# Another order for one attention kernel's engine queues, with PSUM banks named one by one

## The chip, the cores and the metric

The kernel runs on one core of a Trainium2 chip. The metric is device time in microseconds of the whole program. The kernel before takes 495.95 us (median of 3 runs, 495.19 to 496.17).

A core has five engines, each with its own instruction queue that it works off in order. TensorE (PE in the profile) multiplies matrices, and its weight loads are listed as PEld. VectorE (DVE), ScalarE (ACT) and GpSimd (POOL) do the elementwise work. SyncE (SP) only starts DMA transfers here. An engine waits for another by a semaphore. Matrix products land in PSUM, which this kernel holds as eight banks of 128 x 512 float32; everything else lies in SBUF.

## The reference

All data is float32. `x` is 2 x 2048 x 640, the context 2 x 154 x 1024: 77 text rows and 77 image rows per batch. 20 heads of width 32.

```
q    = heads(x @ Wq.T)
k, v       = heads(text @ Wk.T),    heads(text @ Wv.T)
k_ip, v_ip = heads(ip @ Wk_ip.T),   heads(ip @ Wv_ip.T)
out  = softmax(q k.T / sqrt(32)) v  +  softmax(q k_ip.T / sqrt(32)) v_ip
y    = merge(out) @ Wo.T + bo + x
```

The two softmaxes are separate: each row of 154 scores is two rows of 77, each with its own maximum and sum.

## The kernel before

Everything is held transposed, channels on the partitions. The 640 channels are five chunks of 128, and a chunk holds four heads of 32. A chunk of one batch is one `q` number from 0 to 9, and it is cut in two halves of 1024 tokens, so there are 20 units `u`. The 1024 tokens of a unit are eight tiles of 128 tokens, and these are taken in three groups `s` of 3, 3 and 2 tiles (`GROUPS`).

The order of all work is one list, `SCHEDULE`. Each word emits a few instructions, and each engine gets its own in the order of the list. A word is a kind, its numbers and, behind `@`, a place. The kinds that matter here:

- `q.u.h@bank`: the query product of a unit's half block, ten matmul records on line 206; `cq.u.h`: ScalarE copies it out of the bank, scaled (line 220).
- `k.c.t@bank`, `v.c.t@bank`: keys and values of a chunk (line 144); `ck`, `cv` copy them out. `LK.n` loads one block of 512 KB of their weights into slot n modulo 4; weight block n is read by product n, which is 4c + t for k and 4c + 2 + t for v.
- `Rs.u@place`: the scores of group s of unit u (line 242). Four heads run beside each other on 32 rows of the array each, and head g writes bank g of the four that the place names. A three-tile group is 24 matmul records, a two-tile group 16.
- `Ks.u`: ScalarE copies the four banks to SBUF (line 254), head by head. `M`: VectorE's row maxima (line 290, or 293 out of PSUM). `S`: GpSimd subtracts them (line 304). `E`: ScalarE's exponential (line 310). `D`: VectorE's row sums (line 315). `I`: their reciprocals (line 320). `N`: GpSimd multiplies by them (line 325). `T`: VectorE transposes (line 332).
- `A.q@place`: attention times values for a chunk, 160 records on line 341, four banks; `CA.q` copies it out.
- `m`, `o`, `p`, `z`, `F`: products of the output projection (lines 499, 509, 480, 887); `cm`, `co`, `Y`, `yz` add them to sums on VectorE; `G`, `W`, `V`, `X` are sums of operands on GpSimd or VectorE; `SF`, `SS`, `LX`, `LQ`, `LO`, `VS`, `LA`, `LW` are transfers on the sync queue. The projection of the second batch stands at the end of the list, behind A.9.

Three sets say which groups take another way. A group in `BIASED` or `DIRECT` has no subtraction: its exponential is computed row by row on ScalarE, with the negated maximum as a bias (line 278), 24 instructions for a three-tile group and 16 for a two-tile one. A `DIRECT` group is not copied either: its maxima and exponentials read the banks. In `SUMMED` groups the exponentials add up the row sums themselves, and there is no `D`.

Before, the eight banks were two halves of four, and R and A named a half:

```
halves = banks[:G], banks[G:]
...
if k[0] == "R":
    at[name] = halves[int(where)]
    scores(x, i, at[name])
```

In front of the list stand the first loads, five warming matmuls, the query products of units 0 and 2 and the keys of chunk 0, in banks 4, 5, 2 and 7. They are the same in both kernels.

Of the kernel before, what the change touches and what calls it, by code (L numbers as in the profile page):

```python
# [9 lines left out]
F32 = mybir.dt.float32  # L10
# [10 lines left out]
def kernel(  # L21
# [43 lines left out]
        (11, 0), (12, 0), (13, 0), (13, 2), (14, 0), (14, 2), (15, 1), (15, 2), (18, 1), (19, 2),  # L65
    }
    BIASED = {
        (2, 2), (3, 2), (4, 2), (6, 2), (8, 2), (9, 2), (11, 2), (12, 1), (16, 2), (17, 2), (18, 2),
    }
    SUMMED = {  # L70
        (4, 2), (11, 2), (12, 0), (13, 0), (13, 2), (14, 0), (15, 1), (15, 2), (16, 2), (17, 2), (18, 1),
        (18, 2), (19, 2),
# [13 lines left out]
    halves = banks[:G], banks[G:]  # L86
# [183 lines left out]
    def exponential_of(u, s, ps=None, den=None):  # L270

        n = GROUPS[s][1]
        for g in range(G):
            for t in range(n):
                for x in range(2):
                    row = rows_of(u, s)[:, t * G + g, x]
                    one = t * G + g, slice(x, x + 1)
                    nc.scalar.activation(  # L278
                        row,
                        row if ps is None else rows_in(ps[g], n)[:, t, x],  # L280
                        AF.Exp,
                        bias=maxs[(u, s)][:, *one],
                        accum_out=None if den is None else den[:, *one],
                    )
# [300 lines left out]
    for t in range(2):  # L585

        ps = halves[t][G - 2 + t]
        project_kv(t, ps)
        for b in range(B):
            nc.scalar.copy(kT[:, 0, b, t, :], keys_in(ps)[:, b])  # L590
# [73 lines left out]
    def emit(word):  # L664
        name, _, where = word.partition("@")
        k, *args = name.split(".")
        x, y = (*(int(a) for a in args if a.isdigit()), None, None)[:2]
        i = int(k[1:]) if k[1:].isdigit() else None
        if k[0] == "R":
            at[name] = halves[int(where)]  # L670
            scores(x, i, at[name])
        elif k == "A":
            at[name] = halves[int(where)]
# [262 lines left out]
```

## Time and profile before

| | |
|---|---|
| median of 3 runs | 495.95 us (495.19 to 496.17) |
| span of the profiled execution, first to last instruction | 494.6 us (no other time of this execution is given) |
| TensorE busy | 489.1 us, 99% of the span |
| VectorE busy | 413.9 us, 84% |
| GpSimd busy | 370.5 us, 75% |
| ScalarE busy | 309.5 us, 63% |
| DMA | 69.38 MB, mean 140 GB/s |

How to read it: busy times of engines overlap, so only the engine that others wait for sets the time. The chain of waits follows the program back from its last instruction and names at each step what released it. In the rows of that chain a piece is a run of instructions of one line that follow each other without a wait.

### The profile page before, as it was taken

To read this page: it belongs to the slowest core of one execution; us is meant where nothing else is said; L and a number is where in the kernel's file an instruction comes from. 1 tells how busy PE (TensorE), PEld (TensorE's weight loads), DVE (VectorE), ACT (ScalarE), POOL (GpSimd) and SP (SyncE) were. 2 spreads that over 40 slices of the span, in tenths; PEclk is the share of its full clock that TensorE was granted. 3 is DMA by queue.
4 is the path that set the end of the run, shared out by engine and by line. 5 is a ranking of instruction groups with operands and counts; after the bars stand their busy time and mean duration, and the time that the engine had idled before them with its cause. 6 is when DMAs were issued, how large, how long until landed. Compare 5 with 4: busy or idle time off the path is not lost.

```text
span 494.6 us, 10484 instructions
## 1 busy us (share of the span) xinstructions
PE 489.1 (99%) x4116; PEld 287.7 (58%) x4116; DVE 413.9 (84%) x416; ACT 309.5 (63%) x1002; POOL 370.5 (75%) x158
## 2 busy tenths in 40 slices
PE   9999999999999999999999999999999999999997
PEld 5666648558557556456566654754755675444443
DVE  0069989989899989979988896687789898999996
ACT  1275788977687778677899786587889862100000
POOL 0069988988988988879886758475689899798700
PEclk9999999999999999999999999999999999999999
DMA  8992046203241724895540666455550212320125
GB/s 278 350 288 80 17 124 181 67 1 95 62 150 44 247 65 146 270 345 178 161 172 27 215 195 223 134 172 183 184 169 19 90 42 85 129 85 2 42 85 212
DMA packets 67105, 69.38 MB, mean 140 GB/s; under 512 B 5488, under 2 KB 47088, under 8 KB 67056
## 3 DMA queue, kind: packets, MB, share of 16 engines
q1 hardware_dynamic: 66048, 67.54, 43.7%
q10 hardware_dynamic: 1008, 1.18, 0.7%
q8 instruction: 32, 0.52, 0.4%
q14 instruction: 17, 0.14, 0.1%
HBM read 54.94 MB, written 10.49 MB: 132 GB/s over the span
## 4 chain that ended last, share of the span: by engine, by line
PE 96%; DMA 3%; ACTq 0%; ACT 0%; DVE 0%; DVEq 0%; issue 0%
PE bank L206 34%; PE bank L887 12%; PE bank L341 11%; PE bank L242 11%; PE bank L499 10%; PE bank L144 9%; PE bank L480 7%; PE bank L509 3%; DMA aT<-in_L_xattn_Wk_ip_dram 2%; DMA x<-in_x_dram 1%; ACTq L538 0%; ACT pb L254 0%; ACTq L552 0%; DVE acc L830 0%; DVEq L931 0%
## 5 line engine op out<-in xcount | busy, mean ns | idle before, releaser
L325 POOL TENSOR_TENSOR pb<-pb,rden 128x1848 f32<-128x1848 f32 (+1 forms) x60 | 176.0, 2943 | 30.4 <-DVE rden L320 23.6
L304 POOL TENSOR_TENSOR pb<-pb,mx 128x1848 f32<-128x1848 f32 (+1 forms) x39 | 121.6, 3129 | 55.4 <-DVE mx L290 55.3
L206 PE MATMUL bank<-x,wq 128*128 128x512 f32 x280 | 125.4, 598 | 0.1
L332 DVE STREAM_TRANSPOSE pb<-pb 128x1920 f32<-128x1920 f32 (+1 forms) x60 | 115.9, 1938 | 9.1 <-POOL pb L325 8.9
L290 DVE TENSOR_REDUCE mx<-pb 128x24 f32<-128x1848 f32 (+1 forms) x50 | 91.6, 1844 | 32.1 <-ACT pb L254 31.9
L254 ACT COPY pb<-bank 128x462 f32<-128x462 f32 (+1 forms) x200 | 85.3, 542 | 29.3 <-PE bank L242 28.9
L315 DVE TENSOR_REDUCE den<-pb 128x24 f32<-128x1848 f32 (+1 forms) x47 | 88.9, 1895 | 15.6 <-ACT pb L310 12.8
L206 PEld LDWEIGHTS bank<-x,wq 128*128 128x128 f32 x280 | 51.7, 190 | 60.0 <-issue 58.8
L310 ACT ACTIVATE pb<-pb 128x1848 f32<-128x1848 f32 (+1 forms) x39 | 65.6, 1684 | 17.5 <-POOL pb L304 17.4
L278 ACT ACTIVATE pb<-bank,mx 128x77 f32<-128x77 f32 x208 | 60.4, 387 | 6.5 <-DVE mx L293 6.5
L278 ACT ACTIVATE pb<-pb,mx 128x77 f32<-128x77 f32 x184 | 54.1, 356 | 1.9 <-DVE mx L290 1.8
L341 PE MATMUL bank<-pb,v 32*32 32x512 f32 x1600 | 55.2, 597 | 0.0
L206 PE MATMUL bank<-x,aT 128*128 128x512 f32 x116 | 51.8, 596 | 0.0
L242 PEld LDWEIGHTS bank<-kT,qT 32*128 32x128 f32 x1024 | 36.1, 184 | 21.6 <-issue 13.3
L144 PE MATMUL bank<-wo_ct,aT 128*128 128x154 f32 x320 | 46.0, 297 | 0.7 <-DMA aT<-in_L_xattn_Wk_ip_dram 0.4
L144 PEld LDWEIGHTS bank<-wo_ct,aT 128*128 128x128 f32 x320 | 43.0, 188 | 4.7 <-issue 3.0
L242 PE MATMUL bank<-kT,qT 32*128 32x154 f32 x1024 | 45.1, 305 | 0.0
L278 ACT ACTIVATION_READ_ACCUMULATOR pb<-bank,mx 128x1 f32 x168 | 44.0, 266 | 0.0
L341 PEld LDWEIGHTS bank<-pb,v 32*32 32x32 f32 x1600 | 29.0, 103 | 22.7 <-issue 10.1
L480 PE MATMUL bank<-aT,wo_ct 128*128 128x512 f32 x80 | 36.3, 595 | 0.0
L206 PEld LDWEIGHTS bank<-x,aT 128*128 128x128 f32 x116 | 21.4, 190 | 23.7 <-issue 23.5
L220 ACT ACTIVATE qT<-bank 128x512 f32<-128x512 f32 x32 | 19.3, 631 | 23.4 <-PE bank L206 23.4
(83 smaller groups left out, 524.2 us busy)
## 6 DMA issues: line engine op xcount, KB each, us to landing
x<-in_x_dram SPq DMA_DIRECT2D x20, 1280.0 KB, 6.7
out_dram<-acc SPq DMA_DIRECT2D x19, 256.0 KB, 2.9
x<-in_x_dram SPq DMA_DIRECT2D x17, 256.0 KB, 5.9
acc<-in_x_dram SPq DMA_DIRECT2D x16, 256.0 KB, 4.4
out_dram<-x SPq DMA_DIRECT2D x15, 256.0 KB, 2.0
v<-vS SPq DMA_DIRECT2D x160, 20.0 KB, 2.7
aT<-in_L_xattn_Wk_dram SPq DMA_DIRECT2D x5, 512.0 KB, 6.0
aT<-in_L_xattn_Wk_ip_dram SPq DMA_DIRECT2D x5, 512.0 KB, 5.5
```

Source lines behind the costliest of these rows:

```text
L144: nc.tensor.matmul(keys_in(out), loaded[n][:, k, :], cT[:, k, :, t, :], start=(k == 0), stop=(k == NCC - 1))
L206: nc.tensor.matmul(pq, weight_of(q)[:, k, :], xs[place_of(u, h)][:, k, :], start=(k == 0), stop=(k == NC - 1), skip_group_check=loose,)
L242: nc.tensor.matmul(ps[g][:, ts(t, 2 * L)], qTs[(u, h)][g * D : (g + 1) * D, ts(st, P)], kT[g * D : (g + 1) * D, c, b].rearrange("p t l -> ...
L254: nc.scalar.copy(keys_of(u, s)[:, :, g], ps[g][:, : n * 2 * L].rearrange("p (n l) -> p n l", n=n))
L278: nc.scalar.activation(row, row if ps is None else rows_in(ps[g], n)[:, t, x], AF.Exp, bias=maxs[(u, s)][:, *one], accum_out=None if den i ...
L290: nc.vector.tensor_reduce(mx, rows_of(u, s), AX.X, ALU.max, negate=negate)
L304: nc.gpsimd.tensor_tensor(rows_of(u, s), rows_of(u, s), maxs[(u, s)].unsqueeze(3).to_broadcast([P, n, 2, L]), ALU.subtract)
L315: nc.vector.tensor_reduce(den_of(u, s), rows_of(u, s), AX.X, ALU.add)
L325: nc.gpsimd.tensor_tensor(rows_of(u, s), rows_of(u, s), rdens[(u, s)].unsqueeze(3).to_broadcast([P, n, 2, L]), ALU.mult)
L332: nc.vector.transpose(p, p)
L341: nc.tensor.matmul(pa[r][g * D : (g + 1) * D, :], v4s[q % 2][rows, g, k, :], zones[rows, :, g, k, :], start=(k == 0), stop=(k == NK - 1),)
L480: nc.tensor.matmul(ps, wo[:, k, ts(NC - 1, P)], rows_of_attention(b, k)[:, i], start=(k == 0), stop=(k == NC - 1),)
```

## The change

The diff does four things. `SCHEDULE` is another order of the words. R and A name four banks one by one (`R0.0@6452`: head 0 in bank 6, head 1 in 4, head 2 in 5, head 3 in 2) where they named a half. The exponential of a group is four words, one for each head g; for a row-by-row group each emits a quarter of the instructions, for a plain group the first emits the one instruction and the other three emit nothing. And `DIRECT`, `BIASED` and `SUMMED` hold other groups. Pairs of R words next to each other on TensorE go from 14 to 16.

```diff
     DIRECT = {
-        (11, 0), (12, 0), (13, 0), (13, 2), (14, 0), (14, 2), (15, 1), (15, 2), (18, 1), (19, 2),
+        (1, 2), (15, 1), (17, 1), (19, 2),
     }
     BIASED = {
-        (2, 2), (3, 2), (4, 2), (6, 2), (8, 2), (9, 2), (11, 2), (12, 1), (16, 2), (17, 2), (18, 2),
+        (3, 2), (5, 2), (7, 2), (9, 2), (11, 1), (12, 1), (13, 2), (14, 1), (14, 2), (15, 2), (18, 0), (19, 0),
     }
     SUMMED = {
-        (4, 2), (11, 2), (12, 0), (13, 0), (13, 2), (14, 0), (15, 1), (15, 2), (16, 2), (17, 2), (18, 1),
-        (18, 2), (19, 2),
+        (1, 2), (3, 2), (5, 2), (11, 1), (12, 1), (13, 2), (14, 2), (15, 1), (17, 1), (18, 0), (19, 0), (19, 2),
     }
...
-    def exponential_of(u, s, ps=None, den=None):
+    def exponential_of(u, s, g, ps=None, den=None):
...
-        for g in range(G):
-            for t in range(n):
-                for x in range(2):
+        for t in range(n):
+            for x in range(2):
...
-        "q.0.1@5 R0.0@0 cq.0.1 R1.0@1 K0.0 SF.0.0 q.1.0@0 K1.0 M0.0 LK.4 LQ.5 LK.5 M1.0 S0.0 R2.0@1 v.0.0@1 K2.0 "
-        "cq.1.0 S1.0 M2.0 E0.0 v.0.1@5 D0.0 q.1.1@7 LK.7 S2.0 E1.0 LK.6 I0.0 D1.0 N0.0 E2.0 cv.0.0 cv.0.1 R0.1@0 "
-        "I1.0 cq.1.1 D2.0 R1.1@1 K0.1 N1.0 T0.0 k.1.0@0 K1.1 I2.0 M0.1 q.2.1@3 N2.0 T1.0 S0.1 M1.1 R2.1@1 k.1.1@1 "
...
+        "R0.0@6452 q.0.1@7 K0.0 M0.0 cq.0.1 S0.0 q.1.0@2 E0.0.0 E0.0.1 cq.1.0 R1.0@6457 R2.0@0132 K1.0 E0.0.2 "
+        "v.0.1@6 v.0.0@7 K2.0 M1.0 M2.0 S1.0 q.1.1@2 R0.1@5013 E1.0.0 cv.0.0 cv.0.1 cq.1.1 R1.1@4762 K0.1 E0.0.3 "
+        "K1.1 LK.6 SF.0.3 LK.5 k.1.1@5 R2.1@0134 S2.0 D0.0 E2.0.0 E1.0.1 q.3.0@6 E1.0.2 E2.0.1 E1.0.3 I0.0 SQ.0 "
...
+        "LK.12 v.2.0@2 VS.1.0 E0.3.2 cq.5.0 E1.3.1 E0.3.3 K2.4 E1.3.2 E1.3.3 cv.2.0 R1.4@5473 D0.3 R0.4@6012 I2.3 "
...
+        "E0.4.3 E2.4.2 cv.2.1 k.3.1@6 K0.5 D0.4 ck.3.1 E1.4.3 E2.4.3 R2.5@7452 I0.4 D1.4 R1.5@0136 N0.4 SQ.2 I1.4 "
...
         if k[0] == "R":
-            at[name] = halves[int(where)]
+            at[name] = [banks[int(n)] for n in where]
             scores(x, i, at[name])
...
                 elif direct or biased:
-                    exponential_of(
-                        x, i, ps if direct else None, den_of(x, i) if (x, i) in SUMMED else None
-                    )
-                else:
+                    if (x, i) in SUMMED and (x, i) not in dens:
+                        den_of(x, i)
+                    exponential_of(x, i, int(args[1]), ps if direct else None, dens.get((x, i)))
+                elif args[1] == "0":
                     exponential(x, i)
```

More of the change, by code (lines that the diff above doesn't have):

```diff
@@ L85 @@
     banks = [psum.tile([P, TB], F32, name=f"bank_{n}") for n in range(2 * G)]
-    halves = banks[:G], banks[G:]
     wqs = [const.tile([P, NC, P], F32, name=f"wq_{n}") for n in range(3)]
@@ L268, in den_of @@
         return dens[(u, s)]
-    def exponential_of(u, s, ps=None, den=None):
+    def exponential_of(u, s, g, ps=None, den=None):
         n = GROUPS[s][1]
-        for g in range(G):
-            for t in range(n):
-                for x in range(2):
[L276 to L283, printed above, removed]
-                    )
+        for t in range(n):
+            for x in range(2):
+                row = rows_of(u, s)[:, t * G + g, x]
+                one = t * G + g, slice(x, x + 1)
+                nc.scalar.activation(
+                    row,
+                    row if ps is None else rows_in(ps[g], n)[:, t, x],
+                    AF.Exp,
+                    bias=maxs[(u, s)][:, *one],
+                    accum_out=None if den is None else den[:, *one],
+                )
     def maxima(u, s, ps=None, negate=False):
@@ L585 @@
     for t in range(2):
-        ps = halves[t][G - 2 + t]
+        ps = banks[G * t + G - 2 + t]
         project_kv(t, ps)
@@ L669, in emit @@
         if k[0] == "R":
-            at[name] = halves[int(where)]
+            at[name] = [banks[int(n)] for n in where]
             scores(x, i, at[name])
         elif k == "A":
-            at[name] = halves[int(where)]
+            at[name] = [banks[int(n)] for n in where]
             attend(x, at[name])
@@ L701, in emit @@
                 elif direct or biased:
-                    exponential_of(
-                        x, i, ps if direct else None, den_of(x, i) if (x, i) in SUMMED else None
-                    )
-                else:
+                    if (x, i) in SUMMED and (x, i) not in dens:
+                        den_of(x, i)
+                    exponential_of(x, i, int(args[1]), ps if direct else None, dens.get((x, i)))
+                elif args[1] == "0":
                     exponential(x, i)
```

136 rows, old and new, of the table SCHEDULE are left out of this document.

## The prediction, made before the changed kernel was run

> **What bounds the kernel now.** I read the page's busy times first, then the waits of TensorE, then the chain of waits in order of time. The page:
>
> ```profile
> span 494.6 us, 10484 instructions
> PE 489.1 (99%) x4116; PEld 287.7 (58%) x4116; DVE 413.9 (84%) x416; ACT 309.5 (63%) x1002; POOL 370.5 (75%) x158
> ...
> DVE  0069989989899989979988896687789898999996
> ...
> PEclk9999999999999999999999999999999999999999
> ...
> PE 96%; DMA 3%; ACTq 0%; ACT 0%; DVE 0%; DVEq 0%; issue 0%
> ```
>
> The waits of TensorE, all of which lie before the ordered list begins at 19.37 us:
>
> ```profile
> PE bank L573 <- DVE pb L571: 1.1, 1, 1.1
> PE bank L144 <- DMA aT<-in_L_xattn_Wk_ip_dram: 0.4, 1, 0.4
> PE bank L144 <- DMA wo_ct<-in_ctx_dram: 0.3, 1, 0.3
> ```
>
> So the matmul queue sets the end, at full clock, and no other engine matters until TensorE waits for it. What a new order is worth can then come from two things only: how long the same matmuls take in another sequence, and the waits in that sequence. The number of matmuls does not change: both lists hold the same 232 TensorE words (60 R, 10 A, 38 q, 18 k or v, 40 m, o, p and z, 66 F). The chain of waits, by pieces of one line, shows how the sequence matters (start, length, line, records; the record counts are a little short in places):
>
> ```profile
> 19.37 4.29 PE bank L206 x10
> 23.66 1.78 PE bank L242 x48
> 25.45 4.49 PE bank L206 x10
> 29.94 0.74 PE bank L242 x16
> 30.67 4.41 PE bank L144 x32
> 35.09 4.29 PE bank L206 x10
> ...
> 63.21 1.00 PE bank L242 x24
> ...
> 68.69 5.45 PE bank L341 x150
> 74.15 1.00 PE bank L242 x24
> 75.14 4.41 PE bank L144 x32
> 79.56 1.52 PE bank L242 x40
> 81.08 2.31 PE bank L144 x16
> ...
> 210.51 5.45 PE bank L341 x150
> 215.96 4.49 PE bank L206 x10
> ```
>
> L206 is a query word, L242 score words, L144 key and value words, L341 the product with the values. A run of scores costs 0.78 us for each group of three tiles (1.78 − 1.00) and 0.22 us once more for the run (1.00 − 0.78; for two tiles 0.74 is 0.52 + 0.22). A full-width word behind scores costs 0.20 us more than behind another full-width word: 4.49 against 4.29, and 4.41 for two k or v words where the one behind full-width work is 2.10 (4.41 − 2.31). Behind L341 it is the same (215.96 starts where an attention word ends, and takes 4.49). L341 itself is 5.45 us, and scores behind it pay their 0.22 (1.00 at 74.15).
>
> **Part 1, fewer changes between narrow and full-width work: −1.24 us.** I counted neighbours in the two lists. The 60 score words form 46 runs before (14 of them pairs) and 44 after (16 pairs): 2 × 0.22 = 0.44 us. Stretches of full-width words that follow scores or an A word: 50 before (45 behind scores, 5 behind A), 46 after (42 and 4): 4 × 0.20 = 0.80 us. It is more than two pairs alone would give because one more A now stands directly behind scores and one more R directly behind an A. Bounds: −0.84 (only the two pairs count, 0.42 each) to −1.24. I take −1.24, since every row of each kind above has the same price.
>
> **Part 2, waits inside pairs: −0.55 us.** A pair of a two-tile and a three-tile group is 40 records and takes 1.52 us where nothing holds it. Five such pairs take longer:
>
> ```profile
> 91.96 1.74 PE bank L242 x38
> ...
> 129.06 1.74 PE bank L242 x38
> ...
> 166.16 1.75 PE bank L242 x40
> ...
> 228.53 1.67 PE bank L242 x39
> ...
> 273.35 1.76 PE bank L242 x40
> ```
>
> Together that is 0.22 + 0.22 + 0.23 + 0.15 + 0.24 = 1.06 us. In the first three the second group uses the bank of the query word just before the pair (R0.4 after q.5.0@6, R0.6 after q.7.0@6, R0.8 after q.9.0@4), so ScalarE's copy of the queries is not done when the second group comes. The new list names four banks for each word. R2.6@0167 no longer touches the bank of q.7.0@3, but R0.8 still meets that of q.9.0@1, and R2.0 and R1.1 those of q.1.0@2 and q.1.1@2. Nothing in the trace tells how many waits the other banks bring. Bounds: −1.06 (none left) to 0 (as many). I take half.
>
> **Part 3, the beginning: +1.05 us.** Three waits are new, and each is read from the first words of the new list.
>
> First, R0.0 moves ahead of q.0.1. It reads the keys that ScalarE copies from the bank of the last k product:
>
> ```profile
> 19.41 0.35 ACT L590 COPY kT<-bank 128x77 f32<-128x77 f32 x2 [2.47 <-PE bank L144]
> ```
>
> The matmuls are through at 19.37 and the copies at 19.76. Before, q.0.1 covered that (4.29 us); now the whole TensorE queue stands behind R0.0 for 0.4 us (0.3 if the first copy, that of this batch, is enough; 0.5 with a handover).
>
> Second, R1.0 and R2.0 are joined behind q.1.0, and R2.0 needs q.1.0's bank, so cq.1.0 must be done. On ScalarE E0.0 stands ahead of it. R0.0 starting at 19.76 gives K0.0 about 1.9 us of copies (4 × 64.7/136) from 20.85, then the row maximum, the subtraction and the exponential by these rows:
>
> ```profile
> L254 ACT COPY pb<-bank 128x462 f32<-128x462 f32 x136 | 64.7, 590 | 16.6 <-PE bank L242 16.6
> L254 ACT COPY pb<-bank 128x308 f32<-128x308 f32 x64 | 22.1, 440 | 12.7 <-PE bank L242 12.4
> L290 DVE TENSOR_REDUCE mx<-pb 128x24 f32<-128x1848 f32 x34 | 69.5, 2049 | 29.4 <-ACT pb L254 29.3
> L304 POOL TENSOR_TENSOR pb<-pb,mx 128x1848 f32<-128x1848 f32 x33 | 108.3, 3289 | 54.5 <-DVE mx L290 54.5
> L304 POOL TENSOR_TENSOR pb<-pb,mx 128x1232 f32<-128x1232 f32 x6 | 13.5, 2255 | 0.9 <-DVE mx L290 0.8
> L310 ACT ACTIVATE pb<-pb 128x1848 f32<-128x1848 f32 x33 | 58.1, 1765 | 16.7 <-POOL pb L304 16.6
> L220 ACT ACTIVATE qT<-bank 128x512 f32<-128x512 f32 x32 | 19.3, 631 | 23.4 <-PE bank L206 23.4
> ```
>
> 20.85 + 1.9 + 2.05 + 3.29 + 1.77 + 0.63 = 30.49, and 0.1 us of handovers: 30.6. TensorE reaches R2.0 at 19.76 + 1.00 + 4.49 + 4.29 + 0.90 = 30.44. That is 0.15 us of wait (0 to 0.4). The same counting for R1.1 behind cq.1.1 gives 0, with 0.2 as its other end.
>
> Third, the weights of k.1.1. The old list issues LK.4, LQ.5 and LK.5 early; the new one begins its sync queue with LK.6, SF.0.3, LK.5. LK.6 overwrites what v.0.0 reads, so the sync queue, and LK.5 in it, stands until v.0.0 has run. The old list has such loads right behind the v words too (LK.7 and LK.6, issues first, then KB and us to landing):
>
> ```profile
> 35.12 0.37 SPq L134 DMA_DIRECT2D aT<-in_L_xattn_Wv_ip_dram  x1
> 35.54 0.57 SPq L134 DMA_DIRECT2D aT<-in_L_xattn_Wv_dram  x1
> ...
> aT<-in_L_xattn_Wv_ip_dram SPq DMA_DIRECT2D x1, 512.0 KB, 4.2
> ...
> aT<-in_L_xattn_Wv_dram SPq DMA_DIRECT2D x1, 512.0 KB, 5.5
> ```
>
> The first lands 4.2 us after the v words, the second 1.7 us later (35.54 + 5.5 against 35.12 + 4.2), and 256 KB between them is half of that, 0.85. So LK.5 lands 4.2 + 0.85 + 1.7 = 6.75 us after v.0.0. TensorE has q.1.1 (4.29) and the pair R0.1 R1.1 (1.78) in between, 6.07, then k.1.1: a wait of 0.7, or 0.3 if the transfers overlap better. I take 0.5. The sum is 0.4 + 0.15 + 0.5 = 1.05; its ends are 0.6 and 1.8.
>
> **Part 4, what moves under cover: 0.** DIRECT and BIASED groups fall from 21 to 16, all five fewer of two tiles. So GpSimd gets five more subtractions of 2.255 us, 11.3 us, and comes to 381.8 of 494.6. Six more groups are copied by ScalarE (four of three tiles, two of two), about 4 × 1.9 + 2 × 1.4 = 10.4 us (1.4 is 4 × 22.1/64), and for five groups it runs one plain instruction in place of 16 single rows; even with no gain from that it stays at 320, 65%. VectorE has one three-tile sum fewer and two two-tile ones more, less than one reduction of 2.05 us. TensorE's 489.1 covers all three. Without the cover each such microsecond would be one of TensorE's; where that could start is the second rival. Splitting the row-by-row exponentials in four words changes no instruction; the words .1 to .3 of a plain group emit nothing, so its one instruction stands whole at the place of word .0. M0.0 comes about 3.9 us earlier, which gives the softmax engines that much lead.
>
> The five subtractions also meet a rule of the Trainium skill (SBUF — State Buffer, "SBUF: two separate sides"): VectorE and GpSimd share a pair of ports, and an instruction that takes it blocks the other's for its whole length. The subtractions in the trace run 2251/3287/3294 ns (least, median, most) while VectorE is 84% busy, so these forms do not block one another; by the rule each of the five could lose up to one VectorE instruction of 2.05 us, 10 us of GpSimd in all, still inside its 25% of idle time, and the sum stays.
>
> ```profile
> L304 POOL TENSOR_TENSOR pb<-pb,mx x39: 2251/3287/3294, 28.8 to 404.7; 128x1848 f32<-128x1848 f32 x33, 128x1232 f32<-128x1232 f32 x6
> ```
>
> **The sum.** −1.24 − 0.55 + 1.05 = −0.74 us. The profiled span of 494.6 becomes 493.9. The page gives no other time of that execution; the median of the runs, 495.95, is 1.35 us above the span, and I carry this over: **495.2**. The likeliest case's own range, from the bounds, is 495.95 − 1.24 − 1.06 + 0.6 = 494.25 to 495.95 − 0.84 + 1.8 = 496.9.
>
> **The rivals.**
>
> *Cleaner than that.* The early waits are half as long (0.5) and freer banks remove every pair wait: 495.95 − 1.24 − 1.06 + 0.5 = 494.15; with the copies' lead of 3.9 us removing the early wait for cq.1.0 and LK.5 landing in time, 493.4. For it: free choice of four banks out of eight. Against it: the copy wait of R0.0 is in the code.
>
> *Banks that come round too soon.* This one ends slower. The new list has scores that take over banks of the previous scores with one short word between: R1.4 after v.2.0 (banks of R2.4), R2.5 after k.3.1 (R0.5), R0.6 after v.3.0 (R2.6), later R0.17, R1.17, R1.18 and R0.19 after one m word each. A k or v word lasts 2.3 us, the copies of a group 1.4 to 1.9 us. Only 0.4 to 0.9 us is left, and ScalarE has plain exponentials of 1.77 us and row-by-row ones in its queue. As soon as it is over 0.5 us late at these seven places, TensorE waits; with one exponential ahead the wait is 1.77 + 1.9 − 2.3 = 1.4 us. Three of seven so: +4.2, and part 2 gains nothing: 495.95 − 1.24 + 1.05 + 4.2 = 499.95; with one or two of them, 497.2 to 498.6. For it: 84% and 75% on VectorE and GpSimd mean that the copies' successors are seldom early. Against it: ScalarE is idle 37% of the time.
>
> *Joined in name.* The two new pairs, and the attention words beside scores, wait at the second member for as long as they save, like the 1.74 rows: parts 1 and 2 give 0, and 495.95 + 1.05 = 497.0, or 496.4 with the half of part 2.
>
> **How the numbers follow.** About 0.2% (1 us) is what a measurement can tell from no change here: faster is under 494.96, slower over 496.94. Forecast 0.45, cleaner 0.20, banks too soon 0.22, joined in name 0.13. Faster: all of "cleaner" and 0.2 of the forecast, 0.40. Same: 0.23 of the forecast, 0.08 of "joined in name" and 0.04 of "banks", 0.35. Slower: the rest, 0.25. The range 493.4 to 498.4 leaves out the three late copies and what lies below "cleaner".
>
> **What would show it.** R0.0 starting at 19.7 to 19.9 behind an idle gap, and k.1.1 near 42 us behind a wait for a DMA, prove part 3; no gap there disproves it. Part 1: 44 runs of L242, and 4.49 in place of 4.29 four times less. Part 2: pieces of 40 records at 1.52. "Banks too soon" would be waits of TensorE on ScalarE's L254 near R1.4, R2.5 and R0.6, between 95 and 137 us. The forecast is wrong if TensorE has new waits of over 2 us after 60 us, or if the last 70 us, where VectorE has nine tenths of its time filled, get longer.

## The result, and the profile after

The changed kernel takes 521.04 us (median of 4 runs, 519.03 to 522.02); the kernel before took 496.06 us beside it (4 runs, 495.19 to 496.2). The ratio is 1.0499, with a 95% interval of 1.0483 to 1.0516. The forecast was 495.2 us with a range of 493.4 to 498.4, so both the size and the sign were wrong.

In the kernel after, lines are numbered two to fifteen lower or higher: L204 is the query word, L240 scores, L142 keys and values, L338 attention times values, L902 the last products F, L842 and L845 the additions Y and yz, L879 and L881 the sums V, L887 the sums X, L186 a block of x, L158 one copy of the values (VS). The page of the profile after:

```profile
span 519.1 us, 10365 instructions
PE 495.0 (95%) x4116; PEld 292.2 (56%) x4116; DVE 420.5 (81%) x399; ACT 307.3 (59%) x943; POOL 380.9 (73%) x163
...
PEclk9999999999989999979999999999999999999999
...
PE 82%; DVE 10%; DMA 5%; issue 1%; POOL 1%; ACT 0%; ACTq 0%; DVEq 0%; SPq 0%; POOLq 0%
```

TensorE was 99% busy and is 95% busy now, and two slices have a lower clock. The chain of waits has 10% of VectorE in it, where it had 0%. The waits of TensorE (us in total, times, longest); before, there were three in all, of 1.1, 0.4 and 0.3 us:

```profile
PE bank L204 <- DMA x<-in_x_dram: 6.1, 2, 4.8
PE bank L902 <- DVE x L842: 5.7, 3, 3.1
PE bank L240 <- issue: 2.3, 2, 1.5
PE bank L902 <- DVE res L842: 1.5, 1, 1.5
...
PE bank L142 <- ACT pb L252: 1.2, 1, 1.2
...
PE bank L240 <- ACT kT L587: 0.3, 1, 0.3
```

The view puts the wait of k.1.1 (1.2 us, L142) down to ScalarE's copies, which end at 42.39 us. Its weights land at 42.31, so two things end there together; in several of the runs below the view names the load, and with that load issued earlier the wait is gone.

So the time did not go to one thing. To sort it, I gave each TensorE word the price that the rows of before have for it and its neighbours (4.29 and 4.49 us for a query word, 5.45 for attention, 0.86 for a product F, and so on), and listed what each word took beyond that, until the next one began. Before, all words together are 1.7 us over these prices, after 27.5; the prices themselves sum to 1.4 us less, from fewer changes between narrow and full-width work. That leaves 27.5 − 1.7 − 1.4 = 24.4 us, and the spans differ by 519.1 − 494.6 = 24.5. The places are these:

| place (us) | beyond its price | what is seen there |
|---|---|---|
| k.1.1, 41 | 1.3 | its weights land late |
| R0.7 and v.3.1, 149 to 156 | 3.7 | a stop inside R0.7 with no wait, then a low clock |
| R0.9, 188 | 1.3 | such a stop again |
| q.12.1, 222 to 236 | 7.6 | block LX.12.1 lands late (4.9), then a low clock (2.7) |
| q.17.0, 335 | 1.4 | block LX.17.0 lands late |
| A.9, 436 | 0.7 | transpose T2.19 is late |
| last products F, 449 to 487 | 8.7 | VectorE is late |
| pairs of score words | 1.4 | second member waits, as before (1.3) |

They add up to 26.1 us; the rest of the 27.5 is in pieces under 0.15 us.

**The block at 222 us.** The SP queue, after (start, length, line, count) and then before:

```profile
203.88 17.77 SPq L158 DMA_DIRECT2D v<-vS  x24
221.74 0.53 SPq L186 DMA_DIRECT2D x<-in_x_dram  x1
```

```profile
197.17 7.21 SPq L160 DMA_DIRECT2D v<-vS  x8
204.48 0.53 SPq L188 DMA_DIRECT2D x<-in_x_dram  x1
```

The queue takes 17.77 / 24 = 0.74 us to issue each small copy of the values. Before, eight stand ahead of LX.12.1; now there are 24, and the block leaves at 221.74 instead of 204.48. The stretches around it (length, then busy time of TensorE, weight loads, VectorE, ScalarE, GpSimd, then granted clock, share of DMA, GB/s):

```profile
225.00:228.00 3.00, 0.00 (x0) 0.00 (x0) 2.02 (x1) 0.94 (x3) 0.12 (x1) 0.83 1.00 351
228.00:234.00 6.00, 5.75 (x7) 2.52 (x8) 0.06 (x1) 0.00 (x0) 3.28 (x1) 0.52 1.05 371
```

TensorE is idle until 228, and then works for six microseconds at half its clock.

**The stop at 149 us.** TensorE's instructions in order of time, and the granted clock behind them:

```profile
149.38 0.79 PE L240 MATMUL bank<-kT,qT 32*128 32x154 f32 x13
151.69 1.25 PE L240 MATMUL bank<-kT,qT 32*128 32x154 f32 x11 [1.52 <-issue]
```

```profile
150.00:153.00 3.00, 1.48 (x17) 1.00 (x11) 3.00 (x2) 1.65 (x5) 3.00 (x2) 0.81 1.19 302
153.00:157.00 4.00, 4.00 (x22) 4.00 (x23) 2.73 (x3) 1.36 (x4) 1.59 (x2) 0.71 0.23 55
```

R0.7 is one word of 24 matmuls with nothing to wait for between them. After 13 it stands still for 1.52 us, which the view can only call "issue".

**The last stage.** Two stretches that hold the same 310 matmul records, after and before:

```profile
437.00:516.00 79.00, 70.76 (x310) 30.84 (x306) 74.22 (x99) 2.31 (x8) 44.54 (x27) 1.00 0.23 83
```

```profile
422.00:491.00 69.00, 69.00 (x310) 30.83 (x283) 63.44 (x94) 2.31 (x8) 39.65 (x25) 1.00 0.25 89
```

VectorE, the third of the busy times, has about the same number of instructions there, and they take 11 us more. Ten of these are in three forms of sums of 128 x 128 (8.7, 3.2 and 2.5 us, where before they took 2.8, 1.1 and 0.5). VectorE in order of time, then GpSimd in the same stretch:

```profile
436.74 2.09 DVE L881 TENSOR_TENSOR pb<-pb,wo_ct 128x128 f32<-128x128 f32 x1
...
444.54 2.46 DVE L879 SCALAR_TENSOR_TENSOR pb<-pb,wo_ct 128x128 f32<-128x128 f32 x1
447.04 2.32 DVE L881 TENSOR_TENSOR pb<-pb,wo_ct 128x128 f32<-128x128 f32 x1
```

```profile
436.32 2.36 POOL L887 TENSOR_TENSOR aT<-aT 128x1024 f32<-128x1024 f32 x1 [0.62 <-PE bank L506]
...
444.51 4.70 POOL L887 TENSOR_TENSOR pb<-aT 128x1024 f32<-128x1024 f32 x2 [1.18 <-ACT aT L365]
```

These are sums of 128 x 128, and the rows of one form show how far they are from their usual time. In the last stage before, and after:

```profile
L866 DVE TENSOR_TENSOR pb<-pb,wo_ct 128x128 f32<-128x128 f32 x9 | 2.8, 323 | 0.0
```

```profile
L881 DVE TENSOR_TENSOR pb<-pb,wo_ct 128x128 f32<-128x128 f32 x9 | 8.7, 976 | 0.0
```

Each long one began just behind a long sum of GpSimd and ended 0.15 us behind it (436.74 + 2.09 = 438.83, against 436.32 + 2.36 = 438.68). TensorE waits where VectorE is late by that: 3.11 us at F7.1, the largest of the waits on L842.

### The profile page after: what moved, and what is told of

Read it like the earlier page. It is cut to its first block, busy times and chain, and to the rows that moved or that the text cites. A ratio compares the mean times of both kernels' runs of the same rounds, so it can differ in the third digit from the quotient of the medians.

```text
span 519.1 us, 10365 instructions
## 1 busy us (share of the span) xinstructions
PE 495.0 (95%) x4116; PEld 292.2 (56%) x4116; DVE 420.5 (81%) x399; ACT 307.3 (59%) x943; POOL 380.9 (73%) x163
## 4 chain that ended last, share of the span: by engine, by line
PE 82%; DVE 10%; DMA 5%; issue 1%; POOL 1%; ACT 0%; ACTq 0%; DVEq 0%; SPq 0%; POOLq 0%
PE bank L204 34%; PE bank L240 10%; PE bank L338 9%; PE bank L142 9%; PE bank L902 7%; PE bank L496 7%; PE bank L477 3%; DMA x<-in_x_dram 3%; PE bank L506 2%; DVE pb L881 2%; DVE pb L887 2%; DVE x L842 1%; POOL pb L322 1%; DVE pb L329 1%; DMA aT<-in_L_xattn_Wq_dram 1%
## 5 line engine op out<-in xcount | busy, mean ns | idle before, releaser
L301 POOL TENSOR_TENSOR pb<-pb,mx 128x1848 f32<-128x1848 f32 (+1 forms) x44 | 132.9, 3029 | 76.6 <-DVE mx L287 76.5
L287 DVE TENSOR_REDUCE mx<-pb 128x24 f32<-128x1848 f32 (+1 forms) x56 | 102.8, 1854 | 56.8 <-ACT pb L252 56.7
L204 PE MATMUL bank<-x,wq 128*128 128x512 f32 x280 | 128.4, 608 | 6.1 <-DMA x<-in_x_dram 6.1
L329 DVE STREAM_TRANSPOSE pb<-pb 128x1920 f32<-128x1920 f32 (+1 forms) x60 | 114.0, 1924 | 2.7 <-POOL pb L322 2.6
L252 ACT COPY pb<-bank 128x462 f32<-128x462 f32 (+1 forms) x224 | 95.6, 536 | 20.5 <-PE bank L240 20.0
L204 PEld LDWEIGHTS bank<-x,wq 128*128 128x128 f32 x280 | 52.9, 194 | 67.0 <-issue 64.4
L307 ACT ACTIVATE pb<-pb 128x1848 f32<-128x1848 f32 (+1 forms) x44 | 71.0, 1631 | 32.2 <-POOL pb L301 32.1
L275 ACT ACTIVATE pb<-pb,mx 128x77 f32<-128x77 f32 x232 | 74.1, 365 | 2.8 <-DVE mx L287 2.5
L338 PE MATMUL bank<-pb,v 32*32 32x512 f32 x1600 | 55.3, 597 | 0.7 <-DVE pb L329 0.6
L204 PE MATMUL bank<-x,aT 128*128 128x512 f32 x116 | 51.6, 596 | 1.1 <-DMA aT<-in_L_xattn_Wq_dram 1.1
L240 PEld LDWEIGHTS bank<-kT,qT 32*128 32x128 f32 x1024 | 37.9, 185 | 24.0 <-issue 20.2
L240 PE MATMUL bank<-kT,qT 32*128 32x154 f32 x1024 | 46.8, 307 | 2.6 <-issue 2.3
L142 PE MATMUL bank<-wo_ct,aT 128*128 128x154 f32 x320 | 47.1, 301 | 1.2 <-ACT pb L252 1.2
L142 PEld LDWEIGHTS bank<-wo_ct,aT 128*128 128x128 f32 x320 | 44.2, 192 | 5.9 <-issue 3.3
L338 PEld LDWEIGHTS bank<-pb,v 32*32 32x32 f32 x1600 | 29.8, 103 | 22.4 <-issue 9.8
L204 PEld LDWEIGHTS bank<-x,aT 128*128 128x128 f32 x116 | 21.4, 190 | 26.0 <-issue 25.7
L496 PE MATMUL bank<-aT,wo_ct 128*128 128x256 f32 x128 | 32.3, 385 | 0.0
L275 ACT ACTIVATION_READ_ACCUMULATOR pb<-pb,mx 128x1 f32 x160 | 31.9, 199 | 0.0
```

The source lines that it names most:

```text
L142: nc.tensor.matmul(keys_in(out), loaded[n][:, k, :], cT[:, k, :, t, :], start=(k == 0), stop=(k == NCC - 1))
L204: nc.tensor.matmul(pq, weight_of(q)[:, k, :], xs[place_of(u, h)][:, k, :], start=(k == 0), stop=(k == NC - 1), skip_group_check=loose,)
L240: nc.tensor.matmul(ps[g][:, ts(t, 2 * L)], qTs[(u, h)][g * D : (g + 1) * D, ts(st, P)], kT[g * D : (g + 1) * D, c, b].rearrange("p t l -> ...
L252: nc.scalar.copy(keys_of(u, s)[:, :, g], ps[g][:, : n * 2 * L].rearrange("p (n l) -> p n l", n=n))
L275: nc.scalar.activation(row, row if ps is None else rows_in(ps[g], n)[:, t, x], AF.Exp, bias=maxs[(u, s)][:, *one], accum_out=None if den i ...
L287: nc.vector.tensor_reduce(mx, rows_of(u, s), AX.X, ALU.max, negate=negate)
```

## The experiments

The kernels are timed against the kernel before (495.8 to 496.2 us in every comparison). The edits move words of the list or give a sum to another engine (`.d` is VectorE, `.p` GpSimd); the diffs show only the words that matter, for transfers those of the SP queue. In the runs made from the changed kernel the lines behind the list are two lower (L879 here is L881 above), in those made from the kernel before one lower (L865 for L866).

**The block ahead of the copies.**

```diff
-K0.10 E0.9.2 VS.5.0 VS.4.1 VS.5.1 LX.12.1 SF.0.1
+K0.10 E0.9.2 LX.12.1 VS.5.0 VS.4.1 VS.5.1 SF.0.1
```

> Change: in the changed kernel, the load of the token block that q.12.1 reads (LX.12.1) stands ahead of the 24 copies of values (VS.5.0, VS.4.1, VS.5.1) in the sync queue; before it stood behind them. Theory A (the in-order sync queue): the 24 copies took 17.8 us to issue (203.88 to 221.65), so the block load was issued at 221.74 and landed at 228.1, and TensorE waited 4.9 us for it; after that idle time q.12.1 ran at a granted clock of 0.64 and took 7.2 us in place of 4.5. Ahead of them it is issued as soon as q.11.0 has run, some 15 us earlier, so both losses go: 4.9 + 2.7 = 7.6 us less, 513.4 us. Rival (the transfers as such are too many between 200 and 236 us, whatever their order): the wait moves to the copies of values or to the next block, and the time falls by under 3 us. The rival of the prediction (ScalarE's copies of scores come too late) expects no change at this place.

Measured: 520.64 us (519.11 to 524.07), ratio 1.0505 (1.0462 to 1.0548). The expected gain did not come. The wait for x is gone, and another stands in its place:

```profile
217.68 1.04 PE L338 MATMUL bank<-pb,v 32*32 32x512 f32 x2 [1.67 <-DMA v<-vS]
220.21 3.67 PE L338 MATMUL bank<-pb,v 32*32 32x512 f32 x36 [1.49 <-DMA v<-vS]
```

A.4 needs VS.4.1, which still stood behind VS.5.0, and now behind the block too. The two x blocks held the queue from 200.60 to 209.21 (I take it that the slot of LX.12.1 was still being read). The granted clock was 0.50 from 220 to 226 us, now behind A.4's waits. So the low clock goes where the idle time goes.

**The old list with the new order of the copies.** The kernel before, with its two VS.5 words put directly ahead of LX.12.1.

```diff
-SF.0.1 VS.5.0 LX.10.1 VS.4.0 SF.0.4 LX.12.0 LQ.6 VS.4.1 LX.12.1 LO LX.13.0 LX.14.0 VS.5.1
+SF.0.1 LX.10.1 VS.4.0 SF.0.4 LX.12.0 LQ.6 VS.4.1 VS.5.0 VS.5.1 LX.12.1 LO LX.13.0 LX.14.0
```

> Change: the kernel before with one thing of the new order alone: VS.5.0 and VS.5.1 (16 copies of values) are moved to stand directly ahead of LX.12.1 in the sync queue; nothing else moves on any engine. Theory A (the in-order sync queue, with TensorE's slow start after idle time): LX.12.1, issued at 204.5 now, is issued at about 214 to 216 and lands at 220 to 222; q.12.1 wants it at 216, so TensorE waits 4 to 6 us and then runs q.12.1 slowly for 2.5 us more: 502.5 to 504.5 us. Theory B (the wait alone, the slow q.12.1 came from the traffic beside it): 500 to 502. Rival (the copies of values hide behind other work): 496.

Measured: 505.56 us (503.7 to 507.48), ratio 1.0192 (1.0157 to 1.0226). Its SP queue and TensorE:

```profile
198.14 18.36 SPq L160 DMA_DIRECT2D v<-vS  x24
216.59 0.53 SPq L188 DMA_DIRECT2D x<-in_x_dram  x1
```

```profile
222.97 3.49 PE L206 MATMUL bank<-x,wq 128*128 128x512 f32 x4 [5.02 <-DMA x<-in_x_dram]
```

Two words of the list make the old kernel 9.4 us slower. By the same count of prices, 5.1 us are the wait, 1.5 the clock behind it, and 1.9 turned up elsewhere, where the edit was not meant to act: with VS.5.0 gone from its old place, LX.10.1 leaves at 178.00 instead of 188.11, and R0.9 stops inside.

```profile
178.00 0.37 SPq L188 DMA_DIRECT2D x<-in_x_dram  x1
```

```profile
185.80 0.53 PE L242 MATMUL bank<-kT,qT 32*128 32x154 f32 x5 [1.40 <-issue]
```

That is the stop of 149 us again, in a kernel that had none. The packets of the queue named "instruction" between 178 and 183 us, before and in this kernel:

```profile
q8 instruction: 1, 0.02, 1.6%
...
v<-vS SPq DMA_DIRECT2D x1, 20.0 KB, 1.7
```

```profile
q1 hardware_dynamic: 808, 1.42, 87.3%
...
x<-in_x_dram SPq DMA_DIRECT2D x1, 1280.0 KB, 7.5
```

Before, one such packet of 16 KB comes in this stretch (by its own record at 180.07 us); with the block in flight none does (its record has 183.40). Over the whole program the queue moves 32 packets and 0.52 MB, which is 64 bytes for each of TensorE's 8232 matmuls and loads, so I read it as TensorE's own instructions. The places of the stops bear this out: in every run that has them, the stop in R0.7 comes behind 2753 of TensorE's matmuls and loads, and the one in R0.9 behind 3521 or 3522, that is three packets of 16 KB / 64 bytes = 256 instructions further on.

**Fewer loads ahead of the stop.**

```diff
-LX.10.0 LQ.6 LK.16 LK.18 LX.11.1 VS.3.0 VS.3.1
+LK.16 LK.18 LX.10.0 LQ.6 LX.11.1 VS.3.0 VS.3.1
```

> Change: in the changed kernel, two weight loads (LK.16, LK.18, 512 KB each) stand ahead of the block load LX.10.0 in the sync queue in place of behind it, so that they run at about 130 us and not in the burst of 143.9 to 155.7 us. Theory A (TensorE's own instructions are fetched by the same DMA engines, and a 16 KB fetch at 149.28 waits behind that burst): R0.7, which stops in its middle from 149.9 to 151.7 us with no semaphore to wait for, and v.3.1 behind it at a clock of 0.71, lose 3.7 us now and under 1.5 us then: 518.5 us. Rival (a wait for a bank or for weights that the trace does not name): the stop in R0.7 stays, 521 us.

Measured: 519.44 us (518.37 to 520.79), ratio 1.0472 (1.0445 to 1.05). Too little to tell the two apart: LX.10.0 and LQ.6 were still in flight, the packet came at 149.12 us (149.28 in the changed kernel), and R0.7 stopped for 1.42 us.

**No load at all there.**

```diff
-LX.10.0 LQ.6 LK.16 LK.18 LX.11.1 VS.3.0 VS.3.1
+LK.16 LK.18 VS.3.0 LX.10.0 LQ.6 LX.11.1 VS.3.1
```

> The changed kernel, with no load in flight while attend A.2 runs: LK.16 and LK.18 go ahead of LX.10.0, and LX.10.0 and LQ.6 go behind VS.3.0, which waits for the values near 159 us. Theory A (TensorE stops inside R0.7 because the packet with its next instructions waits behind a load): the packet comes near 146 us instead of 149.3, R0.7 takes 1.0 us, v.3.1 2.2 us at full clock: 521.0 - 3.7 = 517.3 us (516.5 to 518.2). Theory B (the stop belongs to the place in the code, or to A.2's short matmuls alone): the stop of 1.4 to 1.5 us stays, and the time is 521.0 us (520.0 to 522.5).

Measured: 518.34 us (517.58 to 520.51), ratio 1.0458 (1.0427 to 1.0488). The time is just over the range of A, and the stop is gone. R0.7 runs in one piece, and the packet now comes between 144 and 149 us, where the changed kernel has none:

```profile
150.12 1.07 PE L240 MATMUL bank<-kT,qT 32*128 32x154 f32 x24
```

```profile
q8 instruction: 1, 0.02, 1.4%
```

By the prices R0.7 and v.3.1 lost nothing (3.7 us in the changed kernel). The last stage lost 11.8 us here instead of 8.7, and q.12.1 and q.17.0 lost 2.4 less, so the time moved by 2.7. The 3.1 us more of the last stage are not the edit's: TensorE ran there from 448 to 455 us at a granted clock of 0.52, behind a wait of 3.2 us, where the changed kernel kept 1.00. The stop is settled: same code, and it comes with the load and goes with it, in both kernels.

**The order of the copies, done rightly.**

```diff
-LX.12.0 VS.5.0 VS.4.1 VS.5.1 LX.12.1 SF.0.1
+LX.12.0 VS.4.1 LX.12.1 VS.5.0 VS.5.1 SF.0.1
```

> The changed kernel, with the second half of the values of step 4 and the block of step 12 (VS.4.1, LX.12.1) taken ahead of both halves of step 5 (VS.5.0, VS.5.1) on SP's queue; all else stays. Theory A (a queue that issues one copy after the other, with the wrong copies in front, and a slow clock that follows the idle time): attend A.4 has its values as before and the block lands near 217 us, so R0.11 to q.12.1 loses its 4.86 us and q.12.1, at a granted clock of 1.00, its 2.73: 521.0 - 7.6 = 513.4 us (512.5 to 514.5). The run that put the block ahead of everything fits A only if its wait went to A.4. Theory B (the clock falls there whatever waits, or a wait of that size turns up at the next user of the queue): 517 us or more, and slices of the granted clock at 0.5 stay between 215 and 240 us.

Measured: 512.44 us (511.52 to 513.6), ratio 1.0333 (1.0308 to 1.0358): 8.6 us less than the changed kernel, where 7.6 were expected; q.17.0's wait (1.4) is absent in this execution too. The queue, and the stretches in which the changed kernel was idle and then slow:

```profile
204.08 6.70 SPq L158 DMA_DIRECT2D v<-vS  x8
211.06 0.37 SPq L186 DMA_DIRECT2D x<-in_x_dram  x1
```

```profile
225.00:228.00 3.00, 3.00 (x8) 1.14 (x6) 1.78 (x1) 1.19 (x3) 0.37 (x1) 1.00 0.35 102
228.00:234.00 6.00, 6.00 (x51) 3.39 (x50) 3.59 (x3) 5.65 (x11) 5.42 (x2) 1.00 0.94 303
```

No idle time, and a clock of 1.00. Theory B is out: the wait didn't move on, and the clock does not fall there of itself.

**Four small sums to GpSimd.** V.R.0, V.U.1, V.O.1 and V.J.0 of the last stage, each one of 2.1 to 2.4 us on VectorE.

```diff
-V.R.0.d  V.U.1.d  V.O.1.d  V.J.0.d
+V.R.0.p  V.U.1.p  V.O.1.p  V.J.0.p
```

> Change: in the changed kernel, four steps of operand sums of the last projection (V.R.0, V.U.1, V.O.1, V.J.0, 128x128 each) run on GpSimd in place of VectorE. In the changed kernel's trace they take 2.09, 2.32, 2.43 and 2.34 us on VectorE, and each ends within 0.2 us of a GpSimd sum of 128x1024 that began before it; their sisters without such a neighbour take 0.28 to 0.54 us. Theory A (the two engines exclude each other for instructions with two SBUF operands): VectorE is free of 9.2 us there, GpSimd gets 4 x 0.5 us, and of the 8.7 us that TensorE waits after the last attention word about 6 go, unless other VectorE sums are caught in their place: 515 us (513 to 518). Rival (VectorE simply has too much to do there): VectorE loses only 4 x 0.4 = 1.6 us of work, and the time falls by at most 1.6 us, 519.4.

Measured: 515.42 us (514.72 to 517.58), ratio 1.0395 (1.0359 to 1.0432): 5.6 us less, the number expected, but not all for the reason expected. By the prices the last products lost 6.3 us instead of 8.7, since other sums were held in place of the four (V.A.0, short in the changed kernel, took 2.43 us at 445.70). Some 2.5 us more are q.17.0's wait and the low clock behind R0.7, which this edit doesn't touch and which are absent in this execution. So the run supports the hold less firmly than its time suggests.

**The same meeting, put into the old kernel.** X.A and X.G, sums of 128 x 1024 that VectorE does in 1.47 us, go to GpSimd.

```diff
-X.A.d@1  X.G.d@0
+X.A.p@1  X.G.p@0
```

> The kernel before, with X.A and X.G (128x1024, 1.47 us each on VectorE) given to GpSimd, where such a sum takes 2.36 us alone; all else stays. It puts the meeting of the changed kernel's last stage into the kernel that has none. Theory A (VectorE's sum is held until GpSimd's ends): of VectorE's small sums of 128x128, all 0.22 to 0.56 us in the kernel before, at least one for each of the two sums goes to 1 to 2.4 us and ends within 0.2 us behind GpSimd's; VectorE loses what it saved (2.9 us) or more, and the time is 496.0 to 500 us. Theory B (no holding; the long durations belong to the changed order's own words): all of them stay under 0.6 us, and the time is 495.5 to 496.5 us.

Measured: 497.94 us (497.32 to 498.52), ratio 1.0034 (1.0024 to 1.0044). VectorE, then GpSimd:

```profile
422.13 2.46 DVE L865 TENSOR_TENSOR pb<-wo_ct,pb 128x128 f32<-128x128 f32 x1
...
425.45 2.47 DVE L865 TENSOR_TENSOR pb<-pb,wo_ct 128x128 f32<-128x128 f32 x1
```

```profile
422.03 2.42 POOL L871 TENSOR_TENSOR x<-aT 128x1024 f32<-128x1024 f32 x1
...
425.34 2.43 POOL L871 TENSOR_TENSOR x<-aT 128x1024 f32<-128x1024 f32 x1
```

Two sums went to GpSimd, and two small ones of VectorE were held, to 0.14 and 0.15 us behind the end of GpSimd's. VectorE has 2.9 us less to do and the program takes 1.9 us more. This is the clearest of the runs: nothing of the changed order is in it. The meeting as such is not new to the old kernel: two sums of 128 x 1024 take 4.76 us together at 430.06 us there, 1.22 and 1.47 being usual, beside a long sum of GpSimd; but no wait of TensorE came of it.

**All mends at once.** The order of the copies, no load at A.2, LK.5 ahead of LK.6, LX.17.0 ahead of SF.2.0, six small sums on GpSimd, V.A.0 ahead of X.D, T2.19 ahead of V.P.1.

```diff
-LK.6 SF.0.3 LK.5 k.1.1@5
+LK.5 LK.6 SF.0.3 k.1.1@5
...
-SS.1.0 LX.17.1 SF.2.0 LX.17.0
+SS.1.0 LX.17.1 LX.17.0 SF.2.0
...
-V.P.1.d V.Q.0.d T2.19 V.R.0.d
+T2.19 V.P.1.d V.Q.0.d V.R.0.p V.R.1.p
```

> The changed kernel with every mend at once: the order of copies, no load beside the fetch at A.2, LK.5 ahead of LK.6, LX.17.0 ahead of SF.2.0, six small sums of the last stage on GpSimd, one on VectorE put earlier, and T2.19 ahead of V.P.1. If the losses are separate and add up: 7.6 + 3.7 + 1.3 + 1.4 + about 8 of the last stage's 9.4 = 22 us less than 521.0, so 499.0 us (496.5 to 502). Still open in it: R0.9 (1.3 us) and the pair waits (about 1.2 us). If the losses have a cause in common that these edits don't touch, or waits move on instead of going, 505 us or more.

Measured: 504.91 us (504.47 to 506.48), ratio 1.0187 (1.0159 to 1.0215), 16.1 us less than the changed kernel and six more than expected. By the prices what was aimed at ahead of 423 us is gone; R0.9 (1.3 us) and the pair waits are left. The last stage lost 7.0 us all the same. The holds had moved: V.U.0 took 2.43 us at 431.26 and V.A.0 2.43 at 433.61, beside GpSimd's X sums. Some 2.6 us of the 7.0 are the clock: behind the wait of 3.7 us that came of it, TensorE had 0.57 from 438 to 446 us.

**Four long sums to VectorE.** To take that away from the other side, X.S, X.U, X.T and X.M go from GpSimd to VectorE in the kernel with all mends.

```diff
-X.S.p@8  X.U.p@4  X.T.p@5  X.M.p@11
+X.S.d@8  X.U.d@4  X.T.d@5  X.M.d@11
```

> The kernel with all mends, and four of GpSimd's long sums of the last stage (X.S, X.U, X.T, X.M) given to VectorE, which has about 4 x 1.2 = 4.9 us more work of its own by that, in a stage where its lateness sets TensorE's waits. Theory A (a sum on VectorE that begins beside a long sum of GpSimd is held until that one ends: in the kernel with all mends V.U.0 2.43, V.A.0 2.43, X.W 2.89 us): these fall to 0.3, 0.3 and 1.2 us, so VectorE has its 4.9 us back from 5.9 us of holds, and the time is 504.9 - 1 to 3 = 502 to 504 us, with no sum of 128x128 above 0.6 us between 428 and 445 us. Theory B (VectorE is late since it has too much work, and the long durations are how the records show that): 508 to 510 us.

Measured: 510.38 us (509.01 to 512.01), ratio 1.0286 (1.0258 to 1.0314). This is the time of B, and the expectation of A failed. Where I had looked, the holds are gone (both sums took 0.28 us). But GpSimd, freed of four sums, comes to the next ones earlier, and these hold later sums of VectorE, with VectorE then above, GpSimd below:

```profile
443.50 2.43 DVE L879 TENSOR_TENSOR pb<-wo_ct 128x128 f32<-128x128 f32 x1
...
446.31 4.75 DVE L885 TENSOR_TENSOR pb<-aT 128x1024 f32<-128x1024 f32 x2
```

```profile
443.38 2.39 POOL L885 TENSOR_TENSOR aT<-aT 128x1024 f32<-128x1024 f32 x1
...
446.20 2.39 POOL L885 TENSOR_TENSOR pb<-aT,pb 128x1024 f32<-128x1024 f32 x1
```

VectorE had 4.9 us more work and some 4 us of new holds (2.43 − 0.28 and 4.75 − 1.22 − 1.47), and TensorE waited 5.5 us at F26.1, and then had a granted clock of 0.57 from 450 to 458 us. The run doesn't refute the hold, since it shows two more; it refutes that one can remove it locally.

**The old last stage in the new order.** The mends ahead of the last stage stay, and the words V, X, F, z, p, Y and yz stand in the order and on the engines of the kernel before, with banks renamed to fit.

```diff
-V.E.0.p ... V.D.0.p ... p.1@4 p.0@5 ... p.2@0 ... A.9@2671 CA.9 ... p.3@3 ... F25.0@1
+V.P.0.p ... V.F.0.d ... p.0@4 p.3@5 ... p.1@0 ... A.9@2671 CA.9 ... p.2@3 F31.1@6
```

> The changed kernel with the mends of the copies, the loads and T2.19, but with the words of the last stage (sums V and X, products F, z, p, additions Y and yz) in the order and on the engines that the kernel before gives them, banks renamed to fit; eight of the sums stand directly ahead of A.9. Theory A (the last stage's loss lies in the order of its own words, that is in which sums of VectorE begin beside long ones of GpSimd): TensorE's waits from F25.0 on, 7.0 us in the kernel with all mends, go to 1 us or less, and the time is 504.9 - 6 to 8 = 497 to 499 us (496.3 to 500). What the change then still loses by are R0.9's stop (1.3 us) and the waits at joined pairs (1.2 us), against 1.4 us that its transitions save. Theory B (VectorE and GpSimd come late to the last stage from the scores of step 19, whatever the order there): TensorE's waits there stay at 4 us or more and the time is 502 us or more.

Measured: 501.91 us (501.18 to 502.31), ratio 1.012 (1.0098 to 1.0142). Between the theories: the last stage lost 3.1 us where it had lost 7.0, 2.6 of them to the clock, which stays at 1.00 here; so more than half of that loss was in the order of its own words. What this stage has beyond the kernel before is again a hold, of V.T.0, on VectorE and GpSimd (the two sums of 4.76 us, here at 435.42, are in both):

```profile
424.31 2.38 DVE L879 TENSOR_TENSOR pb<-pb,wo_ct 128x128 f32<-128x128 f32 x1
```

```profile
424.17 2.37 POOL L885 TENSOR_TENSOR aT<-aT 128x1024 f32<-128x1024 f32 x1 [1.12 <-PE bank L506]
```

In the kernel before, this long sum (X.C) ran at 418.52 us beside the transpose T0.19 (417.77 to 419.95), and neither held the other. Here it met V.T.0. The order of the list alone does not decide it; which two sums meet also depends on when the scores of step 19 end. That the 3.1 us come of this one hold is not tested by a run of its own.

## Why the prediction was wrong

**What bounds the kernel** was right, and the conclusion from it ("What a new order is worth can then come from two things only") too: the prices and the waits. The waits were looked for in the wrong places.

**Part 1, transitions: −1.24 us** forecast; the prices sum to 1.4 us less. Right.

**Part 2, waits inside pairs: −0.55.** Five pairs still pay 0.22 to 0.29 us, with R2.0 1.4 us in all. The 1.06 us of before were a little short: R0.10 and R2.10 waited too, 0.16 us at 203.3 us, where the chain lists the end of the pair as a piece of ScalarE. That makes 1.2 to 1.3, and with every wait of 0.03 us or more counted it is 1.7 after against 1.3 before. So the part is +0.1 to +0.4, outside the bounds of −1.06 to 0: the gain did not come, freer banks changed which pairs pay. From the chain of waits, a pair that pays nothing and two that do:

```profile
58.52 1.52 PE bank L240 x40
...
171.02 1.73 PE bank L240 x39
...
282.63 1.76 PE bank L240 x39
```

**Part 3, the beginning: +1.05.** R0.0 waited 0.31 us for the keys (0.3 to 0.5), R2.0 0.19 (0.15), R1.1 next to nothing. k.1.1 waited 1.19 us where 0.5 was taken and 0.7 was the upper end. The mechanism was right and the size was off: LK.5 landed 6.05 us after its issue at 36.26, and two issues, LK.6 and SF.0.3, had cost 1.05 us ahead of it. With LK.5 in front the wait is gone. The sum, 1.7 us, lies within the bounds (0.6 to 1.8).

**Part 4, "what moves under cover: 0".** This is the step that failed, with some 23 of the 24.5 us. It counted busy time of engines, and that count came out: GpSimd is at 380.9 us (381.8 forecast), ScalarE at 307.3 (at most 320). What it left out were two things for which busy time is no measure.

First, the SP queue. The part costs the edits in the sets DIRECT and BIASED, and no row of it follows a transfer that was moved, beyond the loads of part 3. LX.12.1 went from behind eight copies of values to behind 24. Both rows needed were in the trace of before: 7.21 us for eight copies, and the block that leaves at 204.48 for a word at 216. That block then comes 16 x 0.90 = 14.4 us later by that row (16 x 0.74 = 11.8 by the issue time measured after), and it came 17.3 later, as the copies start later too. Of the rest, the loads that now stand beside A.2 and A.3 could not be costed from before, where TensorE never stops inside a word; it takes the runs to see that a load holds up TensorE's own instructions.

Second, the shared ports. The prediction set a rule on them beside one line of GpSimd, its subtractions, at 2251/3287/3294 ns. From the spread being small it concluded that "these forms do not block one another", and went on as if this held for the kernel. In the score stage VectorE's partners are reductions and transposes with one SBUF input, and no hold shows in this line. The last stage's sums have two, and there VectorE's sum ended 0.14 to 0.15 us behind GpSimd's: 2.46 and 2.47 us in place of 0.28 to 0.55, in the old kernel with two sums moved. VectorE's rows of before showed it already: its sums of 128 x 1024 took from 1.22 to 2.77 us there. The rule is that of the Trainium skill (SBUF — State Buffer, "SBUF: two separate sides"): VectorE and GpSimd share a pair of ports as an exclusive lock, which whoever starts first keeps for the whole instruction; on VectorE's side it concerns instructions in a 2-port mode or with two SBUF inputs, the latter only against a GpSimd one that reads SBUF. The trace agrees to these 0.15 us. The prediction left the condition on the inputs out, and took for its bound a VectorE instruction of 2.05 us, a reduction, which has one. The sentence in the prediction that VectorE had nine tenths of its time filled in the last 70 us was the right place to look; the words V and X ahead of A.9, 14 before and 7 after, were not counted.

**The rivals.** "Banks that come round too soon" comes nearest in time (499.95), but not in mechanism: between 69 and 143 us, where it saw its first waits, TensorE is busy 73.98 of 74.00 us. The slower side was held by a rival in which ScalarE is late; the queue that starts transfers and the ports were in none. What would show the forecast wrong was named rightly, waits of over 2 us after 60 us and a longer last stage, and both came.

**What the change was worth at best.** Its transitions save 1.4 us, and its pairs and R0.0's wait cost some 0.3 each even with LK.5 in time. So with every loss mended it would stand, by this estimate, some 0.8 us below the kernel before. The best run of the new order, 501.91 us, is still 6.1 above (501.91 − 495.8): by the prices R0.9's stop, 1.3, the waits at F20, 2.9, and product m1.3, 1.2, are the larger parts. No run beat the kernel before, and nothing here points to one that would by more than that.

## What to carry to other kernels

When an order changes, follow each transfer and not only each engine: count what stands ahead of it on the queue that issues it, times the issue time (0.74 us a copy here), and compare with the time of its first reader. Then list which instructions of two engines with shared ports will stand beside each other; a rule about ports is to be tested on each pair of forms, and busy shares say nothing on it. And a mend that moves one word shows where the wait goes next, so look at the next reader in the queue before believing the gain.

## What the runs showed of the hardware that I had not expected

- **TensorE's instructions come by DMA, and a load delays them.** 16 KB packets, 32 in the program; where loads of 1280 KB or more were in flight around an attention word (160 short matmuls in 5.5 us), the packet came 2.6 to 3.3 us later than without (149.28 against 146.73, 183.40 against 180.07) and TensorE stopped for 0.67 to 1.52 us, in the middle of a word, with "issue" as the only label. R0.7 without a load there did not stop. Loads do not always do it: near 320 us three were in flight beside A.6, and there was no stop; what decides was not tried.
- **The clock falls after short idle times, and the slow time adds to the wait.** 4.9 us of waiting at q.12.1 were followed by six at a granted clock of 0.52, which cost 2.7 us; 1.52 us of standing still in R0.7 were enough for 0.71 over 153 to 157 us, which cost about 2 us more than the stop, and the 0.79 us in R0.9 were not enough. The Trainium skill (TensorE: Matmul & The Clock Gate, "What's actually happening") says that the clock halves after an idle window of about 3.4 us, one that runs freely, and returns after a busy one. The half clock agrees, and so does the window: the trace records the clock as 1 or 0.5, and in the changed kernel it changes at 151.88, 155.29, 226.97 and 233.80 us, which are 1, 21 and 2 steps of 3.41 us apart. But a step need not be idle throughout. Of the five executions in which R0.7 stopped for 1.3 to 1.5 us, the clock fell in the three in which the whole stop lay in one step, and not in the two in which a step's edge cut it. Among the full-width products of the last stage, 1.9 us of one step did not lower it (changed kernel, 450.37 to 452.25) and 2.1 us did (all mends, 436.54 to 438.64), and 1.66 us at k.1.1 did not (run with the copies done rightly). What else is counted than idle time the runs do not show.
- **Holding is by pairs of sums, and works on either size.** GpSimd's 2.4 us sum holds a VectorE sum of 0.28 us as well as one of 1.2 us; additions that read PSUM beside it keep their time (0.74 us before and after).
